# Graph attention's addend rows through DRAM instead of through TensorE, and layer norms whose squares are summed on ScalarE

## The chip, the cores and the metric

The kernel runs on one core of one Trainium2 chip. The metric is the device time of one execution in microseconds (us), as the median over several executions. No execution quoted here is over 1.5% above the fastest of its kernel, so none counts as slow. Every run was made beside runs of the kernel before on the same chip. A ratio is the mean time of one kernel's fast runs over the mean of the other's of the same rounds, so it is not quite the ratio of the medians that are quoted beside it.

## The reference

64 graphs of 256 nodes with 256 features pass through two layers; all matrices are float32. Cut to what matters here:

```python
# layer 0: two graph attentions, then a feed-forward
Wh = h @ W
e  = leaky_relu(Wh @ a[:F] + (Wh @ a[F:]).T, 0.2)      # one addend per row, one per column
att = softmax(where(adj > 0, e, -9e15), axis=1)
h = att @ Wh                                           # done twice, with W1 and W2
h = layernorm(x + h);  h = layernorm(h + relu(h @ w_ff1 + b1) @ w_ff2 + b2)
# layer 1: attention with relations, then a feed-forward
x = layernorm(h + attention(h) @ Wo + bo)
out = layernorm(x + gelu(x @ W1 + b1) @ W2 + b2)
```

So per graph there are two places where a vector of 256 addends has to lie along the columns, the same in all 128 partitions, and four layer norms.

## The kernel before

The kernel works on 32 pairs of graphs. Each pair's work is a Python generator, and three pairs are under way at once. A rule of turns decides, while the program is built, whose next piece of work is put into the engines' queues. Each `yield us, later, needs` says how long the piece lasts on TensorE, how long its results need before the way can go on, and which of three parts ("gat", "ff", "attention") it needs for itself.

```python
now, going = 0.0, []
while True:
    ...
    able = [g for g in going if alone.get(g[2]) in (None, g[0])]
    ready = [g for g in able if g[1] <= now] or [min(able, key=lambda g: g[1])]
    g = min(ready, key=lambda g: g[2] == "ff" or alone.get("ff") is g[0])
    ...
    us, later, needs = step
    now = max(now, g[1]) + us
    g[1:] = now + later, needs
```

The exponent of a sum is a product of exponentials, so a graph attention's weights need `exp(e1)` and `exp(0.2 e1)` as rows (`rise`) and the other addend as a scalar per partition (`ratio`). Before, the rows are made on TensorE: four transposes of a column that is repeated 128 times.

```python
def gat_weights(y, at, rise, ratio, adjT, empty, b):
    p = bank()
    for n in range(4):
        col = rise[:, n // 2, n % 2:n % 2 + 1]
        nc.tensor.transpose(p[:, n * P:(n + 1) * P], col.to_broadcast([P, P]), ident)   # L225
    up = work.tile([P, N], F32, name="up", bufs=2)
    nc.scalar.activation(up, p[:, :N], AF.Copy)
    ...                                    # VectorE: maximum of the two rows, mask, sums; ScalarE scales y
def add_rows(y, p, b):
    rows = y[:, of_graph(b), :].rearrange("p k d -> p (k d)")
    nc.vector.tensor_tensor(rows, p, rows, ALU.add)
def layernorm(r, gb, b):
    ...
    for j in range(2):
        nc.vector.bn_stats(st[:, j, :], r[:, 2 * b + j, :])
        nc.vector.bn_aggr(mv[:, j, :], st[:, j, :])
    nc.vector.tensor_scalar(rstd, mv[:, :, 1], EPS, None, ALU.add)
    nc.gpsimd.tensor_tensor(rstd, rstd, mhalf[:, :2], ALU.pow)
    ...
```

## Time and profile before

| | before |
|---|---|
| median of 3 runs | 3386.12 us (3384.53 to 3388.64) |
| profiled span | 3384.7 us |
| TensorE busy | 99% |
| VectorE, ScalarE, GpSimd busy | 55%, 40%, 6% |
| pair 1's first matmuls start at | 38.56 us |
| a pair's period in the steady state | 104.06 us |

The last two rows are read from TensorE's timeline, at the matmuls of `xT` with the weights (16 per pair). A pair's period is the distance between these matmuls of pair 3 and of pair 30, divided by 27. The lines of the page, of the waits and of the timelines that carry the argument are shown in the prediction. In all of them PE is TensorE, PEld its weight loads, DVE VectorE, ACT ScalarE, POOL GpSimd and SP SyncE; a letter q behind a name is the engine's sequencer, which hands it its instructions, and L225 is line 225 of that kernel's file. "Granted clock" is the clock that TensorE was given, as a share of full speed.

### The profile page before, as it was taken

Reading aid. Unit: us, or ns where it says so; the run is one execution under the profiler, and the core shown is the slowest. Engines: PE = TensorE matmul, PEld = TensorE weight load, DVE = VectorE, ACT = ScalarE, POOL = GpSimd, SP = SyncE. Lnnn points to the kernel's source line nnn. Section 1 sums busy time; section 2 is a strip of 40 time slices with the busy share of each in tenths; the row PEclk is TensorE's granted clock in tenths of the full one; section 3 lists DMA queues with packets and bytes.
Section 4 is the critical chain, followed back from the end, with each engine's and each line's share of the span. In section 5 each row is a group of like instructions: output and inputs, shape, how many; then the busy total and the mean of one; then the engine's idle time right before and its main releaser. Section 6 shows DMA issues by size and latency. Waiting matters only on the chain.

```text
span 3384.7 us, 46922 instructions
## 1 busy us (share of the span) xinstructions
PE 3335.3 (99%) x18782; PEld 2161.4 (64%) x18782; DVE 1863.3 (55%) x4833; ACT 1366.4 (40%) x2576; POOL 202.8 (6%) x262
## 2 busy tenths in 40 slices
PE   7999999999999999999999999999999999999998
PEld 5656755765676667557656756676576567665755
DVE  5646556556555555565466556555564565565454
ACT  3234434532353254245433542542354335425332
POOL 0000000000000000000000000000000000000000
PEclk9999999999999999999999999999999999999999
DMA  5000100100010001001000100010010001000000
GB/s 170 7 7 26 38 7 9 43 19 13 15 42 14 7 26 38 7 7 44 19 7 13 38 26 7 26 38 7 7 44 19 7 14 38 20 7 19 13 1 14
DMA packets 67296, 78.19 MB, mean 23 GB/s; under 512 B 3712, under 2 KB 58112, under 8 KB 67072
## 3 DMA queue, kind: packets, MB, share of 16 engines
q1 hardware_dynamic: 67072, 75.13, 7.2%
q8 instruction: 150, 2.46, 0.3%
q14 instruction: 74, 0.61, 0.1%
HBM read 58.34 MB, written 16.78 MB: 22 GB/s over the span
## 4 chain that ended last, share of the span: by engine, by line
PE 95%; ACT 4%; DMA 1%; SPq 0%; issue 0%; DVE 0%; POOL 0%; POOLq 0%; DVEq 0%
PE ps L341 26%; PE ps L330 25%; PE ps L364 7%; PE ps L410 7%; PE ps L357 6%; PE ps L382 4%; PE ps L403 4%; PE ps L253 3%; PE ps L427 3%; PE ps L279 3%; PE ps L317 3%; PE ps L267 2%; ACT L215 2%; PE ps L225 1%; ACT L333 1%; ACT xw L269 1%
## 5 line engine op out<-in xcount | busy, mean ns | idle before, releaser
L319 ACT ACTIVATE yT<-ps 128x512 f32<-128x512 f32 x192 | 113.0, 589 | 1069.7 <-PE ps L317 1069.6
L330 PE MATMUL ps<-yT,w_L_gnn_w_ff 128*128 128x512 f32 x1024 | 480.0, 601 | 0.7 <-ACT yT L319 0.7
L330 PE MATMUL ps<-yT,w_L_gnn_W 128*128 128x512 f32 x1024 | 472.4, 596 | 1.4 <-ACT yT L319 1.4
L341 PE MATMUL ps<-w_L_gnn_w_ff,ff 128*128 128x256 f32 x2048 | 458.2, 381 | 0.0
L341 PE MATMUL ps<-w_L_gnn_W,ff 128*128 128x256 f32 x2048 | 456.8, 380 | 0.0
L341 PEld LDWEIGHTS ps<-w_L_gnn_W,ff 128*128 128x128 f32 x2048 | 388.2, 190 | 65.8 <-issue 14.6
L341 PEld LDWEIGHTS ps<-w_L_gnn_w_ff,ff 128*128 128x128 f32 x2048 | 388.1, 190 | 65.8 <-issue 14.3
L396 DVE TENSOR_TENSOR m<-a,adjT 128x512 f32<-128x512 f32 x512 | 327.2, 687 | 175.4 <-ACT a L387 130.3
L302 POOL TENSOR_TENSOR rstd<-rstd,mhalf 128x2 f32<-128x2 f32 x256 | 202.1, 789 | 3175.3 <-DVE rstd L301 3161.6
L387 ACT ACTIVATE a<-ps 128x512 f32<-128x512 f32 x512 | 264.3, 603 | 232.9 <-PE ps L382 232.8
L359 DVE TENSOR_TENSOR v<-ps,b_L_gnn_bv 128x512 f32<-128x512 f32 x128 | 88.1, 689 | 464.4 <-PE ps L357 464.4
L292 DVE TENSOR_TENSOR x<-ps,x 128x512 f32<-128x512 f32 x256 | 175.8, 687 | 265.2 <-PE ps L341 142.1
L333 ACT ACTIVATE ff<-ps,c_L_gnn_b_ff 128x512 f32<-128x512 f32 x256 | 175.9, 687 | 346.0 <-PE ps L330 346.0
L330 PEld LDWEIGHTS ps<-yT,w_L_gnn_W 128*128 128x128 f32 x1024 | 185.3, 190 | 179.0 <-issue 173.7
L330 PEld LDWEIGHTS ps<-yT,w_L_gnn_w_ff 128*128 128x128 f32 x1024 | 182.1, 190 | 178.9 <-issue 175.9
L333 ACT ACTIVATE ff<-ps,c_L_gnn_b 128x512 f32<-128x512 f32 x256 | 175.7, 686 | 148.3 <-PE ps L330 146.7
L357 PE MATMUL ps<-wv,yT 128*128 128x512 f32 x512 | 235.4, 592 | 0.0
L416 DVE RECIPROCAL s<-ps 128x256 f32<-128x256 f32 x128 | 224.0, 1750 | 0.0
L232 DVE SCALAR_TENSOR_TENSOR e<-ps,ratio,up 128x256 f32<-128x256 f32 x256 | 115.8, 475 | 174.0 <-ACT up L227 174.0
L299 DVE BATCH_NORM_STATS2 st<-x 128x6 f32<-128x256 f32 x512 | 192.7, 418 | 8.7
L357 PEld LDWEIGHTS ps<-wv,yT 128*128 128x128 f32 x512 | 97.3, 190 | 122.4 <-issue 122.4
L211 DVE TENSOR_REDUCE steep<-xw 128x1 f32<-128x4 f32 x128 | 19.7, 155 | 256.8 <-ACT xw L269 211.0
(96 smaller groups left out, 4027.6 us busy)
## 6 DMA issues: line engine op xcount, KB each, us to landing
xT<-in_xT SPq DMA_DIRECT2D x32, 512.0 KB, 4.6
adjT<-in_adjT SPq DMA_DIRECT2D x32, 512.0 KB, 3.8
x<-in_x SPq DMA_DIRECT2D x32, 512.0 KB, 4.2
out<-x SPq DMA_DIRECT2D x32, 512.0 KB, 3.2
w_L_gnn_w_ff<-in_L_gnn_w_ff SPq DMA_DIRECT2D x2, 1024.0 KB, 9.4
w_L_gnn_W<-in_L_gnn_W SPq DMA_DIRECT2D x2, 1024.0 KB, 10.3
wv<-in_L_gnn_Wv SPq DMA_DIRECT2D x2, 256.0 KB, 5.0
w_L_gnn_W1T<-in_L_gnn_W1T SPq DMA_DIRECT2D x1, 256.0 KB, 2.8
```

The source lines that it names most:

```text
L292: nc.vector.tensor_tensor(rows, p, rows, ALU.add)
L299: nc.vector.bn_stats(st[:, j, :], r[:, 2 * b + j, :])
L302: nc.gpsimd.tensor_tensor(rstd, rstd, mhalf[:, :2], ALU.pow)
L330: nc.tensor.matmul(p1, lhsT=w1[:, c, m * P:(m + 1) * P], rhs=yT[:, c, :], start=c == 0, stop=c == KC - 1)
L333: nc.scalar.activation(h, p1, func, bias=b1[:, m:m + 1])
L341: nc.tensor.matmul(p2[:, j * D:(j + 1) * D], lhsT=f[m][:, k * P:(k + 1) * P], rhs=w2[:, m, :], start=m == 0, stop=m == NF - 1)
L357: nc.tensor.matmul(ps, lhsT=yT[:, c, at:at + P], rhs=wv[:, c].rearrange("p r m -> p (r m)"), start=c == 0, stop=c == KC - 1)
L364: nc.tensor.matmul(ps, lhsT=w[:, d, c * P:(c + 1) * P], rhs=yT[:, d, :], start=d == 0, stop=d == KC - 1)
L387: nc.scalar.activation(a, ps[o], AF.Exp)
L396: nc.vector.tensor_tensor(m, a, adj, ALU.mult)
L410: nc.tensor.matmul(po[o * DH:(o + 1) * DH, :N], lhsT=v[:, jc, at:at + DH], rhs=ms[o][:, jc * N:(jc + 1) * N], start=r == 0 and jc == 0, st ...
L416: nc.vector.reciprocal(s, po[:, N:])
```

## The change

The intent is to take 512 transposes and their wait off TensorE. The four exponentials of a pair are laid into 32-column blocks, VectorE transposes the blocks, a DMA of 4 KB writes them to DRAM as one row, and a second DMA of 512 KB reads that row back into all partitions. Both are issued by GpSimd. The layer norms change too: the row additions give the sums for the means, and ScalarE sums the squares. The pauses in the rule of turns are fitted to the new chain, the next pair's loads are put into the queue in layer 2 instead of layer 1, a pause precedes the last store of each pair, and `x` gets a fifth buffer.

```diff
-        nc.tensor.transpose(p[:, n * P:(n + 1) * P], col.to_broadcast([P, P]), ident)   (and the copy to up)
+        blocks = small.tile([P, 2, 32], F32, name="blocks")
+        nc.vector.transpose(blocks..., rise...)
+        row = scratch.tile([2, 16, 32], F32, name="row")                                  # in DRAM
+        nc.gpsimd.dma_start(row.rearrange("j q c -> q j c"), blocks[0:P:8])
+        rows = work.tile([P, 8, 4, 32], F32, name="rows")
+        nc.gpsimd.dma_start(rows..., row....partition_broadcast(P))
...
-            a.append(addends(y, D + 2, 0, pair, b))
-            yield 1.75, b * 1.6, None
...
-            e.append(gat_weights(y, D + 2, *a.pop(0), adjT, empty, b))
-            yield 0.5, b * 4.4, None
+            if b == 0:
+                yield 1.75, 0.0, None
+        rows, ratio = addends(y, D + 2, 0, pair)
+        yield 1.75, 8.6, None
+        e = [gat_weights(y, D + 2, rows, ratio, adjT, empty, b) for b in range(2)]
+        yield 0.0, 4.6, None
...                                                        (layer 2 likewise)
-        nc.vector.tensor_tensor(rows, p, rows, ALU.add)
+            nc.vector.scalar_tensor_tensor(row, p[...], 1.0, row, op0=ALU.mult, op1=ALU.add, accum_out=sums[:, j:j + 1])
+        nc.vector.tensor_scalar(nm, sums, -1.0 / D, None, ALU.mult)
...
-            nc.vector.bn_stats(...); nc.vector.bn_aggr(...)
+            nc.scalar.activation(aside, r[:, 2 * b + j, :], AF.Square, bias=nm[:, j:j + 1], accum_out=square[:, j:j + 1])
```

More of the change, by code (lines that the diff above doesn't have):

```diff
@@ L61, in load @@
         nc.sync.dma_start(adjT, t["adjT"][rows].rearrange("b (c p) n -> p (b c) n", p=P))
-        x = io.tile([P, 4, D], F32, name="x", bufs=4)
+        x = io.tile([P, 4, D], F32, name="x", bufs=5)
         nc.sync.dma_start(x, t["x"][rows].rearrange("b (c p) d -> p (b c) d", p=P))
@@ L76, in two_layers @@
     most = const.tile([P, NPAIR, 4], F32, name="most")
-    steep = const.tile([P, NPAIR, 4], F32, name="steep")
+    steep = const.tile([P, NPAIR, 2], F32, name="steep")
+    rises = [const.tile([P, 2, 32], F32, name=f"rise{n}") for n in range(2)]
+    for rise in rises:
+        nc.vector.memset(rise, 0.0)
     def weights(name, pool=const):
@@ L145, in two_layers @@
     small = ctx.enter_context(tc.tile_pool(name="small", bufs=6))
+    scratch = ctx.enter_context(tc.tile_pool(name="scratch", bufs=4, space=bass.MemoryType.DRAM))
     psum = ctx.enter_context(tc.tile_pool(name="psum", bufs=8, space=bass.MemoryType.PSUM))
@@ L204, in of_graph, with addends, gat_weights @@
         return slice(2 * b, 2 * b + 2)
-    def addends(y, at, layer, pair, b):
-        k = of_graph(b)
-        nc.vector.tensor_reduce(steep[:, pair, 2 * layer + b:2 * layer + b + 1], y[:, k, at:at + 2], axis=AX.XY,
-                                op=ALU.max, apply_absolute_value=True)
-        e1, e2 = y[:, k, at], y[:, k, at + 1]
-        rise, ratio = small.tile([P, 2, 2], F32, name="rise"), small.tile([P, 2], F32, name="ratio")
-        nc.scalar.activation(rise[:, 0], e1, AF.Exp, bias=shift[:, 0:1])
-        nc.scalar.activation(rise[:, 1], e1, AF.Exp, bias=shift[:, 0:1], scale=ALPHA)
-        nc.scalar.activation(ratio, e2, AF.Exp, scale=ALPHA - 1.0)
-        return rise, ratio
-    def gat_weights(y, at, rise, ratio, adjT, empty, b):
-        p = bank()
-        for n in range(4):
-            col = rise[:, n // 2, n % 2:n % 2 + 1]
-            nc.tensor.transpose(p[:, n * P:(n + 1) * P], col.to_broadcast([P, P]), ident)
-        up = work.tile([P, N], F32, name="up", bufs=2)
-        nc.scalar.activation(up, p[:, :N], AF.Copy)
+    def addends(y, at, layer, pair):
+        nc.vector.tensor_reduce(steep[:, pair, layer:layer + 1], y[:, :, at:at + 2], axis=AX.XY, op=ALU.max,
+                                apply_absolute_value=True)
+        rise, ratio = rises[layer], small.tile([P, 4], F32, name="ratio")
+        of_kind = rise.rearrange("p j (n s) -> p n j s", n=4)[:, :, :, 0]
+        for b in range(2):
+            e1 = y[:, of_graph(b), at]
+            nc.scalar.activation(of_kind[:, 2 * b], e1, AF.Exp, bias=shift[:, 0:1])
+            nc.scalar.activation(of_kind[:, 2 * b + 1], e1, AF.Exp, bias=shift[:, 0:1], scale=ALPHA)
+        nc.scalar.activation(ratio, y[:, :, at + 1], AF.Exp, scale=ALPHA - 1.0)
+        blocks = small.tile([P, 2, 32], F32, name="blocks")
+        nc.vector.transpose(blocks.rearrange("p j c -> p (j c)"), rise.rearrange("p j c -> p (j c)"))
+        row = scratch.tile([2, 16, 32], F32, name="row")
+        nc.gpsimd.dma_start(row.rearrange("j q c -> q j c"), blocks[0:P:8])
+        rows = work.tile([P, 8, 4, 32], F32, name="rows")
+        nc.gpsimd.dma_start(rows.rearrange("p q n c -> p (q n c)"), row.rearrange("j q c -> (j q c)").partition_broadcast(P))
+        return rows, ratio
+    def gat_weights(y, at, rows, ratio, adjT, empty, b):
         e = work.tile([P, 2, N], F32, name="e", bufs=4)
@@ L231, in gat_weights @@
             k = 2 * b + j
-            nc.vector.scalar_tensor_tensor(e[:, j], p[:, N:], ratio[:, j:j + 1], up, op0=ALU.mult, op1=ALU.max)
+            nc.vector.scalar_tensor_tensor(e[:, j].rearrange("p (q c) -> p q c", q=8), rows[:, :, 2 * b + 1],
+                                           ratio[:, k:k + 1], rows[:, :, 2 * b], op0=ALU.mult, op1=ALU.max)
             nc.vector.scalar_tensor_tensor(e[:, j], adjT[:, k], empty[:, k:k + 1], e[:, j],
@@ L246, in gat_layers @@
         z = work.tile([P, 4, D + 4], F32, name="xw", bufs=2)
-        a, e = [], []
         for b in range(2):
@@ L255, in gat_layers @@
                 nc.scalar.activation(y[:, k], ps[:, :D + 4], AF.Copy)
-            a.append(addends(y, D + 2, 0, pair, b))
-            yield 1.75, b * 1.6, None
-        if pair + 1 < NPAIR:
-            loaded[pair + 1] = load(pair + 1)
-        for b in range(2):
-            e.append(gat_weights(y, D + 2, *a.pop(0), adjT, empty, b))
-            yield 0.5, b * 4.4, None
+            if b == 0:
[4 more added lines that the diff above has]
+        yield 0.0, 4.6, None
         for b in range(2):
@@ L269, in gat_layers @@
                 nc.scalar.activation(z[:, 2 * b + i, :D + 2], ps[:, :D + 2], AF.Copy)
-            a.append(addends(z, D, 1, pair, b))
-            yield 1.75, 0.4 + b * 0.6, None
-        for b in range(2):
-            e.append(gat_weights(z, D, *a.pop(0), adjT, empty, b))
-            yield 0.5, b * 4.4, None
+            if b == 0:
+                yield 1.75, 0.4, None
+        rows, ratio = addends(z, D, 1, pair)
+        if pair + 1 < NPAIR:
+            loaded[pair + 1] = load(pair + 1)
+        yield 1.75, 8.6, None
+        e += [gat_weights(z, D, rows, ratio, adjT, empty, b) for b in range(2)]
+        yield 0.0, 4.6, None
         for b in range(2):
@@ L280, in gat_layers @@
                                      rhs=z[:, 2 * b + j, :D], start=j == 0, stop=j == 1)
-            add_rows(x, ps, b)
-            layernorm(x, ln[0], b)
+            layernorm(x, add_rows(x, ps, b), ln[0], b)
             if b == 0:
@@ L289, in add_rows, with layernorm @@
     def add_rows(y, p, b):
-        rows = y[:, of_graph(b), :].rearrange("p k d -> p (k d)")
-        nc.vector.tensor_tensor(rows, p, rows, ALU.add)
-    def layernorm(r, gb, b):
+        sums, nm = small.tile([P, 2], F32, name="rowsum"), small.tile([P, 2], F32, name="nm")
+        for j in range(2):
+            row = y[:, 2 * b + j, :]
+            nc.vector.scalar_tensor_tensor(row, p[:, j * D:(j + 1) * D], 1.0, row, op0=ALU.mult, op1=ALU.add,
+                                           accum_out=sums[:, j:j + 1])
+        nc.vector.tensor_scalar(nm, sums, -1.0 / D, None, ALU.mult)
+        return nm
+    def layernorm(r, nm, gb, b):
         g, beta, _ = gb
-        st, mv = small.tile([P, 2, 6], F32, name="st"), small.tile([P, 2, 2], F32, name="mv")
-        rstd = small.tile([P, 2], F32, name="rstd")
+        square, rstd = small.tile([P, 2], F32, name="square"), small.tile([P, 2], F32, name="rstd")
         for j in range(2):
-            nc.vector.bn_stats(st[:, j, :], r[:, 2 * b + j, :])
-            nc.vector.bn_aggr(mv[:, j, :], st[:, j, :])
-        nc.vector.tensor_scalar(rstd, mv[:, :, 1], EPS, None, ALU.add)
+            aside = work.tile([P, D], F32, name="aside", bufs=2)
+            nc.scalar.activation(aside, r[:, 2 * b + j, :], AF.Square, bias=nm[:, j:j + 1],
+                                 accum_out=square[:, j:j + 1])
+        nc.vector.tensor_scalar(rstd, square, 1.0 / D, EPS, ALU.mult, ALU.add)
         nc.gpsimd.tensor_tensor(rstd, rstd, mhalf[:, :2], ALU.pow)
@@ L304, in layernorm @@
             row = r[:, 2 * b + j, :]
-            nc.vector.scalar_tensor_tensor(row, row, mv[:, j, 0:1], g, op0=ALU.subtract, op1=ALU.mult)
+            nc.vector.scalar_tensor_tensor(row, row, nm[:, j:j + 1], g, op0=ALU.add, op1=ALU.mult)
         for j in range(2):
@@ L344, in feed_forward @@
                     if j == 1:
-                        add_rows(y, p2, b)
-                        layernorm(y, gb, b)
+                        layernorm(y, add_rows(y, p2, b), gb, b)
                     yield 3.44, 0.0, None
-        add_rows(y, p2, 1)
-        layernorm(y, gb, 1)
+        layernorm(y, add_rows(y, p2, 1), gb, 1)
         done_with("ff")
@@ L428, in into_rows @@
                                      start=c == 0, stop=c == KC - 1)
-            add_rows(y, ps, b)
-            layernorm(y, ln[2], b)
+            means.append(add_rows(y, ps, b))
+        means = []
         groups = [(b, c) for b in range(2) for c in range(KC)]
@@ L456, in attention @@
             divided(b, c, po)
+            if last:
+                layernorm(y, means[0], ln[2], 0)
             yield 3.1 if last else 4.1, 4.8 if last else 0.8, None
@@ L468, in attention @@
         into_rows(1)
+        layernorm(y, means[1], ln[2], 1)
         done_with("attention")
@@ L485, in whole_way @@
         yield from feed_forward(x, ff1, AF.Gelu, ln[3])
+        yield 3.44, 5.0, None
         nc.sync.dma_start(out[2 * pair:2 * pair + 2].rearrange("b (c p) d -> p (b c) d", p=P), x)
-        yield 3.44, 0.0, None
     in_turn((whole_way(pair) for pair in range(NPAIR)), 3)
-    ranges = ((reach, NPAIR * 4, N * SAFE), (most, NPAIR * 4, 1.0), (steep, NPAIR * 4, STEEP))
+    ranges = ((reach, NPAIR * 4, N * SAFE), (most, NPAIR * 4, 1.0), (steep, NPAIR * 2, STEEP))
     count = const.tile([P, len(ranges)], F32, name="count")
```

## The prediction

> **What bounds the kernel now.** I read the busy line of the page first, then the chain that ended last, then TensorE's waits, then the start and the end in the timeline.
>
> ```profile
> PE 3335.3 (99%) x18782; PEld 2161.4 (64%) x18782; DVE 1863.3 (55%) x4833; ACT 1366.4 (40%) x2576; POOL 202.8 (6%) x262
> ...
> PE 95%; ACT 4%; DMA 1%; SPq 0%; issue 0%; DVE 0%; POOL 0%; POOLq 0%; DVEq 0%
> ```
>
> TensorE is busy in all but 49.4 of 3384.7 us and carries 95% of the chain; no other engine is above 55%. A matmul's record overlaps the next one's, so busy alone does not prove a bound; the waits do:
>
> ```profile
> PE ps L225 <- ACT rise L215: 19.4, 23, 0.9
> PE pw L117 <- DVE junk L111: 7.3, 1, 7.3
> PE ps L253 <- DMA xT<-in_xT: 5.1, 1, 5.1
> PE ps L279 <- ACT xw L238: 3.3, 1, 3.3
> PE ps L267 <- ACT xw L238: 2.6, 1, 2.6
> ```
>
> Columns: total us, times, longest. All but the first line happen once, in the first 40 us; one more, 2.1 us at the first feed-forward, is left out here. So in the steady state the only thing TensorE ever waits for is the exponentials ahead of the four transposes that make the addend rows (L225). The kernel is bound by TensorE's amount of work; everything else hides behind it. So of this change only three things count: TensorE work taken away, the wait taken away, and any new wait.
>
> ```profile
> L292 DVE TENSOR_TENSOR x<-ps,x 128x512 f32<-128x512 f32 x256 | 175.8, 687 | 265.2 <-PE ps L341 142.1 <-PE ps L279 112.5 <-PE ps L427 10.1
> ...
> L299 DVE BATCH_NORM_STATS2 st<-x 128x6 f32<-128x256 f32 x512 | 192.7, 418 | 8.7
> ...
> L238 ACT ACTIVATE xw<-xw,rs 128x258 f32<-128x258 f32 (+1 forms) x256 | 115.8, 500 | 20.8 <-DVE rs L235 18.9
> ...
> L300 DVE BATCH_NORM_AGGREGATE mv<-st 128x2 f32<-128x6 f32 x512 | 77.6, 173 | 0.0
> ...
> L225 PE MATMUL ps<-ident,rise 128*128 128x128 f32 x512 | 71.3, 275 | 19.4 <-ACT rise L215 19.4
> ...
> L418 DVE SCALAR_TENSOR_TENSOR junk<-ps,s 128x256 f32<-128x256 f32 x128 | 54.3, 424 | 3.8
> ...
> L227 ACT ACTIVATE up<-ps 128x256 f32<-128x256 f32 x128 | 42.3, 379 | 3.5 <-PE ps L225 3.5
> ```
>
> ```profile
> x<-in_x SPq DMA_DIRECT2D x32, 512.0 KB, 4.2
> ```
>
> These rows (busy us, mean ns, idle before; below them a DMA's row, KB and us to landing) are the prices used below. For the start, the first pair has nothing to hide behind, and the timeline of TensorE shows it bare:
>
> ```profile
> 28.05 5.41 PE L279 MATMUL ps<-xw,e 128*128 128x256 f32 x16 [3.29 <-ACT xw L238]
> 38.56 5.38 PE L253 MATMUL ps<-w,xT 128*128 128x260 f32 x16 [5.10 <-DMA xT<-in_xT]
> ...
> 44.76 0.65 PE L225 MATMUL ps<-ident,rise 128*128 128x128 f32 x4 [0.37 <-ACT rise L215]
> 45.25 3.68 PE L157 MATMUL ps<-c_L_gnn_b_ff2c,w_L_gnn_w_ff 128*128 128x1 f32 x32
> ...
> 62.17 1.04 PE L225 MATMUL ps<-ident,rise 128*128 128x128 f32 x8
> 63.05 5.32 PE L330 MATMUL ps<-yT,w_L_gnn_w_ff 128*128 128x512 f32 x12
> ```
>
> ```profile
> 12.00:24.00 12.00, 8.81 (x44) 6.88 (x42) 4.91 (x20) 8.19 (x26) 0.00 (x0) 1.00 1.03 327
> 24.00:40.00 16.00, 7.49 (x23) 5.73 (x24) 11.63 (x38) 2.80 (x9) 1.73 (x2) 0.84 1.01 285
> 40.00:60.00 20.00, 18.94 (x84) 14.12 (x83) 8.02 (x24) 8.85 (x26) 0.00 (x0) 0.78 0.41 128
> ```
>
> The last three columns of the windows are granted clock, DMA share and GB/s: until 40 us the weights fill the DMA engines, and after idle stretches the clock falls below 1.
>
> **What the Trainium skill says.** "DMA: Bandwidth & Descriptors", section "Anatomy of one DMA — SWDGE (gpsimd) path", puts a DMA from GpSimd at about 2.0 us + bytes/436 GB/s. This kernel has none of that kind; its 512 KB loads from SyncE land in 3.8 to 4.6 us, against 3.2 us by that line, so I add one microsecond to it. The same page, "Two DMAs through the same engine are not ordered", says that a DMA reading what another wrote has to wait for the other's semaphore: the two new ones come one after the other. "ScalarE: Activation LUTs", "What ACT_TABLE_LOAD costs", gives 280 + 0.833 N ns for an ACTIVATE with a per-partition operand, 493 ns for N = 256; L238 agrees with 500 ns, and the trace's table loads agree with its 1283 ns. "TensorE: Matmul & The Clock Gate", "Part 1: The HAM clock gate", says that idle windows of about 3.4 us halve the clock; the 0.84 and 0.78 above agree.
>
> **The change part by part.**
>
> *Addend rows.* The 512 transposes and their weight loads go. The 71.3 us of the row overlap with neighbours, so I count from start to start: eight take 63.05 - 62.17 = 0.88 us, four alone 45.25 - 44.76 = 0.49 us. Summed over the whole timeline, up to the next other matmul and without waits, it is 61.2 us (between 64 x 0.88 = 56 and 128 x 0.49 = 63). With the 19.4 us of wait, 80.6 us of TensorE's time. Pair 0 lies in the start, which I count apart: 61.2 x 31/32 = 59.3, and 19.4 less its 0.31 + 0.37 = 18.7, together 78.0 us for pairs 1 to 31.
>
> In their place, once per layer and pair: five small exponentials, a block transpose on VectorE, a 4 KB DMA to DRAM, and a 512 KB broadcast back. Length of that chain after the last xw matmul, by the rows before: ACT copy 0.4, perhaps 0.3 behind other work, perhaps a table load 1.28, four exponentials at 0.2 apart 0.9, transpose about 0.3 (an estimate: 64 columns beside the 0.16 us of the smallest VectorE operations), DMA 2.0 to 2.5, broadcast 3.2 + 1 to 5: landing at 9 to 11 us. Then 2.7 us (VectorE's first row at 16.81 to TensorE at 19.55 us in the first pair) until TensorE can go on: 12 to 14 us.
>
> What lies beside it? I followed the kernel's rule of turns, old and new, only for the order of issue. In layer 1, between the new addends and the matmuls that need them stand five feed-forward blocks of four matmuls (4 x 0.433 = 1.73 us each) and two of sixteen (16 x 0.216 = 3.45): 8.7 us up to the VectorE part and 15.6 us in all. In layer 2 it is over 30 us. So the 12 to 14 us fit, with 1.6 us to spare at worst. VectorE is reached at 8.7 us and may stand in its queue until the rows land, 1 to 2 us; but there only the feed-forward runs, whose TensorE work needs no VectorE. Slip in the steady state: 2 us in all as my estimate, for 31 pairs mostly none.
>
> *Start.* Pair 0 has no cover. Before, the last xw matmul ended at 15.5 and the next matmuls began at 19.56. Now: rise 16.8, transposed 17.1, row written about 19.8, broadcast back about 25 (DMA engines full in this stretch, so 5 us), TensorE at 27.8. Second layer: matmuls until 32.5 at a lowered clock, +1.5 to rise, +0.3, DMA 2.5, broadcast 4, +2.7: 43.5 instead of 28.05. These end near 48.5, and pair 1's matmuls follow at once, for its xT, landed at 38.5, is there; before they began at 38.56. Start: +10 us, of which the lowered clock is 2.
>
> *Layer norm.* VectorE loses 192.7 + 77.6 + 175.8 us and gains 512 additions with a sum at 424 + 81 ns (the price of L418 and its accumulator read; some overlap, 0.47 apart, 241 us) and 256 small ones at 0.16 (41 us): about 160 less, to 1700. ScalarE gains 512 squares at 0.493 us, 252 us, loses 42 of `up` and some exponentials: near 1560 us, 46%, if the square needs no table of its own. None of that is on TensorE's path. The chain of one norm: before 4.0 us; now 0.94 + 0.2 + 1.1 + 0.2 + 0.8 + 0.9 = 4.2 and a hop more between engines, perhaps 4.6. The kernel leaves 6 us after each norm, so only the last ones show: +0.4 in the tail and +0.6 where the last pair has no cover.
>
> Sum: 3386.1 - 78.0 + 10 + 1 + 2 = 3321. The rounder picture, all gains and a start of only +8 with no slip, gives 3317. I put 3320.
>
> **Rivals.** (1) *A new wait in the place of the old one*: the rows land after 13 us in each pair's layer 1. Each microsecond of it costs 31 us in all; 1 us makes 3350, 2.5 us eats the gain. For it: two dependent transfers and a queue on GpSimd that also carries the norms' powers. Against: 15.6 us of cover and the diff's own pauses of 8.6 and 4.6, which look fitted. I give 15% to more than 0.5 us per pair. (2) *ScalarE becomes the brake*: squares queue ahead of evictions that TensorE needs, or the square forces table loads (512 x 1.28 us would be 657 us more). Against: 40% busy now, and TensorE never waits for ScalarE's evictions today beyond 2.1 us at L330 in the start. A few us at most; 3% for the table case, which would end near or above the old time. (3) *The norms on GpSimd wait behind the DMAs*: POOL's queue stands about 2 us between the DMAs; by the order of issue a norm follows closely only after layer 2's addends, with 4 us to the use after its own 4. Costs nothing, I think.
>
> **Range and chances.** The gain is bounded at 3386.1 - 80.6 = 3305.5. Below 3307 is hardly reachable; upward a slip of 0.6 us per pair gives 3340. So 3307 to 3340 for 8 in 10. The 2% line is near 3319, almost on my figure: faster 0.45, same 0.52, slower 0.03.
>
> **What would show it.** L225 gone, and with it the first line of the waits; PE busy near 3335 - 61 = 3274; no repeated TensorE wait on ACT xw for rows; TensorE's first pair stretched to about 48 us before pair 1; two GpSimd DMAs, 64 each, the broadcast landing in 4 to 5 us; VectorE waiting for rows 1 to 2 us per layer; squares near 0.5 us; no more table loads than 208. I am wrong if matmuls of L267's kind wait in most pairs, if pair 1 starts later than 52 us, or if ACT stands before the feed-forward's second half.

## The result, and the profile after

The kernel after takes **3364.82 us** (median of 6 runs, 3363.33 to 3366.6) beside 3386.24 us of the kernel before: ratio 0.9937, 95% interval 0.9924 to 0.995. It is faster, but by 21 us (less than 1%) in place of 66, and the time is far outside the range of 3307 to 3340.

The page of the kernel after, its busy line and its chain that ended last:

```profile
PE 3288.1 (98%) x18270; PEld 2105.2 (63%) x18270; DVE 1699.7 (51%) x4835; ACT 1524.4 (45%) x3350; POOL 275.5 (8%) x390
...
PE 78%; DVE 10%; DMA 6%; ACT 3%; issue 2%; POOL 1%; DVEq 0%; POOLq 0%; ACTq 0%
```

TensorE lost 47.2 us of busy time, and the 512 transposes are gone. But the chain now runs through VectorE, the DMAs and ScalarE for a fifth of its length; before, 95% of it was TensorE. TensorE's waits in the kernel after (total us, times, longest) say where:

```profile
PE ps L274 <- ACT xw L247: 18.5, 1, 18.5
PE ps L289 <- ACT xw L247: 14.2, 1, 14.2
...
PE ps L394 <- ACT kT L377: 6.4, 10, 2.4
PE ps L355 <- ACT ff L347: 3.7, 9, 0.7
```

The first two happen once each, in the first pair. The other two are of a kind that the kernel before did not have outside its start: TensorE waits for results of ScalarE, 19 times in all. The waits at L225, the largest of the kernel before, are gone.

The trace splits into three stretches. The predicted figures are the prediction's own: a start of 48.5, then 3336.9 us as before less 78.0, plus 2 of slip and 0.6 for the last pair, then 9.2 us as before plus 0.4.

| us | before | predicted | after | after less predicted |
|---|---|---|---|---|
| up to pair 1's first matmuls | 38.6 | 48.5 | 59.7 | +11.2 |
| from there to the start of TensorE's last matmul | 3336.9 | 3261.5 | 3287.0 | +25.5 |
| from there to the end | 9.2 | 9.6 | 14.9 | +5.3 |
| profiled span | 3384.7 | 3319.6 | 3361.6 | +42.0 |

Some 2 us more lie between the profiled run, which was the fastest of its kernel, and the median. Each of the three rows has another cause.

**The start.** TensorE's timeline in the kernel after, to be held against that of before in the prediction (start, length, line, and in brackets the idle time ahead):

```profile
34.15 5.60 PE L274 MATMUL ps<-xw,e 128*128 128x258 f32 x16 [18.52 <-ACT xw L247]
53.99 5.89 PE L289 MATMUL ps<-xw,e 128*128 128x256 f32 x16 [14.24 <-ACT xw L247]
59.72 3.67 PE L261 MATMUL ps<-w,xT 128*128 128x260 f32 x16
```

And GpSimd's timeline in the same stretch:

```profile
17.16 0.67 POOL L229 DMA_DIRECT2D row<-blocks  x1 [15.83 <-DVE blocks L227]
22.90 0.59 POOL L231 DMA_DIRECT2D rows<-row  x1 [5.07 <-DMA row<-blocks]
41.26 0.52 POOL L229 DMA_DIRECT2D row<-blocks  x1 [17.77 <-DVE blocks L227]
47.06 0.56 POOL L231 DMA_DIRECT2D rows<-row  x1 [5.28 <-DMA row<-blocks]
```

GpSimd waited 5.07 and 5.28 us for a row of 4 KB. The broadcast of layer 1, issued at 22.90, came to VectorE's first use at 31.39 us, 8.5 us later; that of layer 2, issued at 47.06, at 51.23 us. Over the whole run the page has medians of 1.9 and 3.9 us for the same two DMAs. In this stretch the DMA engines are full (a share of 1.09 from 41 to 47 us too), and TensorE's clock falls (window of the kernel after from 24 to 40 us; the last three columns are granted clock, DMA share and GB/s):

```profile
24.00:40.00 16.00, 5.60 (x16) 4.27 (x16) 4.85 (x18) 3.56 (x10) 0.00 (x0) 0.56 1.03 302
```

**The middle.** The periods of the pairs are not all alike. From pair 3 to pair 18 they are about 102.0 us, 2.0 less than before, close to the 2.5 that the prediction took (78.0 / 31). From pair 21 to pair 29 they are about 103.3, with one of 107.7. The order of TensorE's work shows why. Pair 10 first, then pair 25, both in the kernel after (L261 opens a pair, L344 and L355 are the two halves of a feed-forward of another pair, L274 is the first layer's attention):

```profile
971.43 3.67 PE L261 MATMUL ps<-w,xT 128*128 128x260 f32 x16
974.94 8.75 PE L344 MATMUL ps<-yT,w_L_gnn_w_ff 128*128 128x512 f32 x20
983.52 7.07 PE L355 MATMUL ps<-w_L_gnn_w_ff,ff 128*128 128x256 f32 x32
990.43 1.90 PE L274 MATMUL ps<-xw,e 128*128 128x258 f32 x8
```

```profile
2513.28 3.67 PE L261 MATMUL ps<-w,xT 128*128 128x260 f32 x16
2516.79 8.75 PE L344 MATMUL ps<-yT,w_L_gnn_w_ff 128*128 128x512 f32 x20
2525.37 10.52 PE L355 MATMUL ps<-w_L_gnn_w_ff,ff 128*128 128x256 f32 x48
2535.73 1.90 PE L274 MATMUL ps<-xw,e 128*128 128x258 f32 x8
```

The same five blocks of four, but then 48 matmuls in place of 32 before the attention may go on. The diff has the reason in it: the new pause is 8.6 us, and a block counts 1.72 us in the rule of turns. Five blocks are exactly 8.6. So "the pause is over" and "now" are one moment, and `g[1] <= now` is decided by the rounding of two long sums. Up to pair 20 it came out true; past a nominal time of about 2048 us, where the spacing of the numbers doubles, it came out false, and the pair goes on one block later. Running the rule alone on a computer, with the pauses of this kernel, gives the same: at pair 20 (nominal 1982 us) the pause ends 2e-13 us before "now", at pair 21 (2085 us) 9e-13 us after it. I call the two orders the first and the second.

What the second order costs is seen on ScalarE. The same place in pairs 10 and 25: the attention's rows have just been transposed, and the feed-forward's last activation (L347) is due.

```profile
1051.63 0.51 ACT L313 ACTIVATE aside<-x,nm 128x256 f32<-128x256 f32 x1 [5.90 <-DVE nm L305]
...
1053.11 0.67 ACT L347 ACTIVATE ff<-ps,c_L_gnn_b 128x512 f32<-128x512 f32 x1
```

```profile
2589.80 0.51 ACT L313 ACTIVATE aside<-x,nm 128x256 f32<-128x256 f32 x1 [6.15 <-DVE nm L305]
...
2593.55 0.51 ACT L313 ACTIVATE aside<-x,nm 128x256 f32<-128x256 f32 x1 [2.64 <-DVE nm L305]
...
2594.65 1.28 ACT L347 ACT_TABLE_LOAD   x1
2595.95 0.69 ACT L347 ACTIVATE ff<-ps,c_L_gnn_b 128x512 f32<-128x512 f32 x1
```

In the first order one norm's squares stand ahead of the activation, in the second the squares of two norms. ScalarE takes its work in order. So the activation waits until the second pair of squares has had its means from VectorE (2.64 us), and behind them for a load of its table (ACT_TABLE_LOAD, 1.28 us) which the first order does not need here: the kernel after has 150 table loads, experiment 1 with the first order throughout has 128. TensorE shows the cost. Its 16 matmuls at this place (L355, from 2593.81 us) take 4.48 us up to the next ones, against 3.45 in pair 10, with a wait of 0.36 us at 2597.75 inside, and the transposes ahead of them (L331) 0.25 us more: 1.28 us in all, nearly all of the 1.3 to 1.4 that a period of the second order is longer. In the single period of 107.7 us TensorE also waits 2.41 us for `kT` from ScalarE; after that wait the granted clock is 0.5 for 3.4 us, and four matmuls take 3.68 us in place of 1.98.

**The end.** The last output is issued at 3351.04 us, and the program ends 10.5 us later; before, from 3379.63 us, it took 5.1. The trace has the reason among the records that are not counted as busy: GpSimd's closing DRAIN, which starts once its work is done.

```
GpSimd's closing DRAIN, start us and ns:   before 3379.0   45      after 3350.22   10522
```

### The profile page after: what moved, and what is told of

Same layout as the page of the kernel before. It is cut to its first block, busy times and chain, and to the rows that moved or that the text cites.

```text
span 3361.6 us, 46862 instructions
## 1 busy us (share of the span) xinstructions
PE 3288.1 (98%) x18270; PEld 2105.2 (63%) x18270; DVE 1699.7 (51%) x4835; ACT 1524.4 (45%) x3350; POOL 275.5 (8%) x390
## 4 chain that ended last, share of the span: by engine, by line
PE 78%; DVE 10%; DMA 6%; ACT 3%; issue 2%; POOL 1%; DVEq 0%; POOLq 0%; ACTq 0%
PE ps L355 24%; PE ps L344 21%; PE ps L369 6%; PE ps L376 5%; PE ps L422 4%; PE ps L394 3%; PE ps L261 3%; PE ps L274 3%; DMA adjT<-in_adjT 3%; DVE m L408 2%; PE ps L415 2%; PE ps L439 2%; DVE s L428 2%; PE ps L289 2%; DMA rows<-row 2%
## 5 line engine op out<-in xcount | busy, mean ns | idle before, releaser
L313 ACT ACTIVATE aside<-x,nm 128x256 f32<-128x256 f32 x512 | 255.4, 500 | 695.3 <-DVE nm L305 578.2
L344 PE MATMUL ps<-yT,w_L_gnn_W 128*128 128x512 f32 x1024 | 471.6, 597 | 0.7 <-ACT yT L333 0.7
L355 PE MATMUL ps<-w_L_gnn_W,ff 128*128 128x256 f32 x2048 | 462.5, 380 | 4.6 <-ACT ff L347 3.7
L355 PE MATMUL ps<-w_L_gnn_w_ff,ff 128*128 128x256 f32 x2048 | 455.2, 379 | 0.0
L344 PE MATMUL ps<-yT,w_L_gnn_w_ff 128*128 128x512 f32 x1024 | 452.2, 594 | 0.7 <-ACT yT L333 0.7
L355 PEld LDWEIGHTS ps<-w_L_gnn_w_ff,ff 128*128 128x128 f32 x2048 | 389.0, 190 | 66.6 <-issue 15.1
L355 PEld LDWEIGHTS ps<-w_L_gnn_W,ff 128*128 128x128 f32 x2048 | 382.8, 190 | 62.4 <-ACT ff L347 11.5
L303 DVE SCALAR_TENSOR_TENSOR x<-ps,x 128x256 f32<-128x256 f32 x512 | 196.7, 413 | 338.9 <-PE ps L355 290.2
L344 PEld LDWEIGHTS ps<-yT,w_L_gnn_w_ff 128*128 128x128 f32 x1024 | 192.6, 191 | 217.7 <-issue 207.9
L344 PEld LDWEIGHTS ps<-yT,w_L_gnn_W 128*128 128x128 f32 x1024 | 183.7, 190 | 185.7 <-issue 176.2
L240 DVE SCALAR_TENSOR_TENSOR e<-rows,ratio 128x256 f32<-128x256 f32 x256 | 116.4, 477 | 333.3 <-DMA rows<-row 309.9
L347 ACT ACTIVATE ff<-ps,c_L_gnn_b_ff 128x512 f32<-128x512 f32 x256 | 175.6, 687 | 206.9 <-PE ps L344 206.9
L347 ACT ACTIVATE ff<-ps,c_L_gnn_b 128x512 f32<-128x512 f32 x256 | 173.1, 684 | 83.6 <-PE ps L344 82.2
L247 ACT ACTIVATE xw<-xw,rs 128x258 f32<-128x258 f32 (+1 forms) x256 | 117.4, 502 | 160.1 <-DVE rs L244 160.1
```

Source lines behind the costliest of these rows:

```text
L303: nc.vector.scalar_tensor_tensor(row, p[:, j * D:(j + 1) * D], 1.0, row, op0=ALU.mult, op1=ALU.add, accum_out=sums[:, j:j + 1])
L313: nc.scalar.activation(aside, r[:, 2 * b + j, :], AF.Square, bias=nm[:, j:j + 1], accum_out=square[:, j:j + 1])
L344: nc.tensor.matmul(p1, lhsT=w1[:, c, m * P:(m + 1) * P], rhs=yT[:, c, :], start=c == 0, stop=c == KC - 1)
L347: nc.scalar.activation(h, p1, func, bias=b1[:, m:m + 1])
L355: nc.tensor.matmul(p2[:, j * D:(j + 1) * D], lhsT=f[m][:, k * P:(k + 1) * P], rhs=w2[:, m, :], start=m == 0, stop=m == NF - 1)
```

## The experiments

Twelve kernels ran, in four batches, each on another chip. Each gave correct results. The kernel before had medians of 3385.19 to 3385.99 us in the batches and 3386.24 beside the kernel after, so a difference between kernels of different batches is uncertain by about 1 us more than the spread of each.

**1. The order of turns kept.** The equality is decided by a margin, nothing else is changed.

```diff
-            ready = [g for g in able if g[1] <= now] or [...]
+            ready = [g for g in able if g[1] <= now + 1e-6] or [...]
```

> The changed kernel with one edit to its rule of turns: a way counts as ready at now + 1e-6 instead of now, so that two moments that are equal but for rounding stay equal and the order of issue of pairs 3 to 20 holds to the end. Theory (order): the trace of the changed kernel shows a period of 101.9 us for pairs 3 to 18, 107.7 us once at pair 22 and 103.3 us for pairs 23 to 28; with one order all through, 10 x 1.35 + 4.4 = 18 to 20 us go, 3364.8 to about 3346 us, and every period from pair 3 on is 101.8 to 102.3 us. Rival (wear of some other kind, or the DMAs): the later periods stay at 103.3 us and the time within 3 us of 3364.8.

Measured: **3347.83 us** (3346.66 to 3349.4), ratio 0.9888, that is 17.0 us less than after. Its period is 102.02 us: 102.05 up to pair 18, 101.89 from pair 21. Of TensorE's waits for ScalarE almost nothing is left:

```profile
PE ps L394 <- ACT kT L377: 0.6, 1, 0.6
...
PE ps L355 <- ACT ff L347: 0.5, 1, 0.5
```

**2. The norms alone**, in the kernel before.

> The kernel before with the new layer norms alone (sums with the additions, squares on ScalarE, the first norm of attention moved). Theory (rows and start make the loss): within 3 us of 3386, as predicted, for TensorE's work is the same and the norms hide. Rival (ScalarE is the brake): 10 to 30 us slower, with TensorE waiting for ff or yT from ScalarE in most periods.

Measured: 3387.22 us, ratio 1.0004 (0.999 to 1.0018). The new norms neither gain nor cost there: in the steady state TensorE waits for nothing there but the exponentials of the rows, so the 148 us that VectorE saves there (1863.3 to 1715.3) have no taker.

**3. The rows alone**: the kernel after with the old norms, and with the flip of the order still in it.

> The changed kernel with the old layer norms (bn_stats and bn_aggr on VectorE) in the new places; the order of issue with its flip at pair 21 stays. Theory (start, order, end): start and end cost the same; in the second order the wait of 0.36 us for ff goes, for no square stands ahead of it, so 3355 to 3365. Rival (the norms eat the gain): 3340 or less.

Measured: 3347.76 us (3344.89 to 3349.65), ratio 0.9888. I had expected 3355 to 3365 by the theory and 3340 at most by the rival, so both numbers were missed. What it says is that the second order by itself costs little: with the old norms no squares stand in ScalarE's queue, and from pair 23 to 28 the period is 102.08 us, against 101.69 with the first order (experiment 12). The table loads are 150 here too. But ScalarE runs this one long before its activation:

```profile
2571.40 1.28 ACT L342 ACT_TABLE_LOAD   x1
2580.36 0.69 ACT L342 ACTIVATE ff<-ps,c_L_gnn_b 128x512 f32<-128x512 f32 x1 [7.68 <-PE ps L339]
```

So neither the order nor its extra table loads are enough: the 16 matmuls take 3.46 us here, and only the 0.25 us at the transposes ahead of them stay. The loss of 17 us needs both, the order and the squares.

**4. A single DMA from GpSimd** in the kernel before, read by nobody.

```diff
+    nc.gpsimd.dma_start(aside.tile([P, DH], F32, name="unread"), ones)
```

> The kernel before with a single DMA from GpSimd's queue at the start that nobody waits for. Theory (end): using GpSimd's queue at all makes the end of the program longer, 10.5 us instead of 5.1 from the issue of the last output to the last instruction, so about 5 us more, 3391 us. Rival (the end is long because of how many such DMAs there were, or by chance): within 1 us of 3386.

Measured: 3386.34 us, ratio 1.0002. GpSimd's closing DRAIN takes 140 ns. So the longer end does not come from the mere use of GpSimd's queue.

**5. Pair 0 by transposes.** To experiment 1, pair 0's rows are added in the old way, by TensorE; with this code pair 1's loads go back to their old place too.

```diff
+        e = yield from (first_layers(y, z, xT, adjT, empty) if pair == 0 else rest_layers(...))
```

> The kernel of e1_ties with pair 0 alone made by transposes on TensorE as before, all other pairs by block transpose and DMAs. Theory (start): in e1_ties pair 1's first matmuls begin at 61.9 us, before the change at 38.6; with pair 0's rows made on TensorE they begin at 38.5 to 41 us, so 19 to 22 us go: about 3327 us, with the same periods of about 102.0 us. Rival (the start's waits only move work that is waited for later, such as the weights): less than 10 us, with new TensorE waits between 40 and 110 us.

Measured: **3328.01 us** (3326.12 to 3328.55), ratio 0.9827. Pair 1 starts at 38.08 us, as in the kernel before and 23.9 us sooner than in experiment 1; 19.8 us of that show in the median. The closing DRAIN, with 124 DMAs in place of 128, takes 10.196 us: 0.0815 us less for each one, which makes 10.4 us for 128 of them. So the drain grows with the number of DMAs issued.

**6. A quiet start, first try.** To experiment 1: seven large weights, 4.75 MB, should be loaded only after pair 0's second layer. A memset of one column on VectorE was to hold each load back.

> The kernel of e1_ties with 4.75 MB of weights (both feed-forwards, Wq, Wk, Wo) loaded only after pair 0's layer 2 weights are made, so that pair 0's row DMAs do not share the DMA engines with them. Theory (start = two dependent DMAs beside the weight loads): the four DMAs of pair 0's rows, 5.1, about 8, 5.3 and 4 us to landing in the changed kernel, fall to about 2 and 4; pair 1's first matmuls begin at 46 to 53 us instead of 61.9; the time falls by 8 to 14 us, less what TensorE then waits for the weights of the first feed-forward (up to 5 us). Rival (the start is long because of the chain's fixed latency and the clock): the DMAs stay long and pair 1 begins at 58 us or later.

Measured: 3349.78 us, ratio 0.9894; pair 1 starts at 62.51 us. The edit did not do what it was for. A memset depends on nothing, so all seven ran at 1.1 us, and the loads went out from 21.9 us on. The run says nothing of the theory; experiment 9 mends it.

**7. The row DMAs from SyncE's queue**, on top of experiment 5.

```diff
-        nc.gpsimd.dma_start(row...)    nc.gpsimd.dma_start(rows...)
+        nc.sync.dma_start(row...)      nc.sync.dma_start(rows...)
```

> The kernel of e5_ties_start with the two row DMAs of each layer issued from SyncE's queue and not from GpSimd's. Theory (end): GpSimd's last drain lasts 10.52 us in the changed kernel, 0.14 with one GpSimd DMA and 0.05 without, about 0.08 us per DMA issued there; with none it is 0.05 us again and the program ends 5 us sooner than e5_ties_start, about 3322 us. The periods stay at about 102.0 us, unless loads and outputs hold the rows up in SyncE's queue. Rival (the drain belongs to the program, not to the number of GpSimd DMAs): the end stays at 10 us after the last output's issue.

Measured: **3324.65 us** (3322.79 to 3328.0), ratio 0.9818. GpSimd's drain is back at 45 ns, and from the last output's issue to the end it is 5.09 us in place of 10.38. So the longer end is the drain. Of that 5.3 us 3.4 show in the median, and the runs of the two experiments overlap (3322.79 to 3328.0 beside 3326.12 to 3328.55): that the whole gets faster by it is likely, not shown. The two DMAs land in 1.7 and 3.5 us, against 1.8 and 3.8.

**8. The second order throughout.** In the kernel after, the first pause is lengthened by a tenth of a microsecond, so the order of pair 25 holds from pair 3 on.

```diff
-        yield 1.75, 8.6, None
+        yield 1.75, 8.7, None
```

> The changed kernel with the pause after the addends of layer 1 at 8.7 instead of 8.6, nothing else: by the rule of turns the second order of issue then holds from pair 3 on. Theory (order): the period of 103.3 us, seen in the changed kernel for pairs 23 to 28 alone, holds from pair 3 on: 18 more periods at 1.2 to 1.4 us more, so 3382 to 3392 us, no gain over the kernel before (the 4.4 us of the change of order may go). Rival: within 4 us of 3365.

Measured: **3387.72 us**, ratio 1.0004: a nominal tenth of a microsecond, of which no engine ever hears, takes the whole gain. The period is 103.53 us. TensorE's waits for ScalarE now come in nearly every pair:

```profile
PE ps L394 <- ACT kT L377: 12.9, 24, 1.7
PE ps L355 <- ACT ff L347: 9.5, 26, 0.4
```

**9. A quiet start, second try.** As 6, but the column is copied from pair 0's second exponentials, so the loads must wait for them.

```diff
-            nc.vector.memset(tile_[:, 0, :1], 0.0)
+            nc.vector.tensor_copy(tile_[:, 0, :1], e[3][:, 0, :1])
             nc.sync.dma_start(tile_, w...)
```

> The kernel after with the order of turns kept, and with seven of the large weights (4.75 MB) issued only after pair 0's second layer has its exponentials: each weight tile's first column is first written by a copy that reads those exponentials, so the queue of SyncE really stands still until then. The earlier try at this used a memset, which depends on nothing and ran at 1.1 us. Theory: the row DMAs of pair 0 were slow (5.1, about 8, 5.3, about 4 us) because the weights and the prefetch behind them fill the DMA engines. Then layer 2's two DMAs fall to about 1.9 and 3.9 us, layer 1's to between that and what they were (pair 0's and pair 1's loads are still there), pair 1's first matmuls start at 47 to 54 us in place of 61.9, and the whole takes 3334 to 3342 us if the feed-forward's weights then come in time (a wait of some us at the first feed-forward would give part of it back). Rival: the two DMAs from GpSimd are slow in the start whatever else runs (a cold queue, say): start of pair 1 at 58 us or later and 3344 us or more.

Measured: 3348.23 us, ratio 0.989; pair 1 starts at 57.96 us. This time the weights were held until 52.67 us. GpSimd's timeline shows layer 2's row in a quiet stretch, and TensorE's wait for it:

```profile
43.18 0.52 POOL L234 DMA_DIRECT2D row<-blocks  x1 [16.20 <-DVE blocks L232]
45.35 0.56 POOL L236 DMA_DIRECT2D rows<-row  x1 [1.65 <-DMA row<-blocks]
```

```profile
PE ps L298 <- ACT xw L252: 10.3, 1, 10.3
```

The wait for layer 2's row fell from 5.04 us (experiment 1) to 1.65, and from transposed blocks to VectorE's first use it is 6.3 us in place of 9.7. The DMA engines' share is 0.01 from 43 to 46 us here, and 0.88 from 44 to 49 us in experiment 1. So in layer 2 the 4 KB row was slow because of what ran beside it; the rival, that DMAs from GpSimd are slow in the start whatever else runs, falls. The broadcast gained nothing (3.87 us to the first use, 3.86 in experiment 1). Layer 1 was not relieved: the loads of pairs 2 to 4 moved up into the gap, the row waited 6.52 us there, and TensorE 18.4 as before. My figure for the whole was missed. Of the 4 us gained at pair 1, 2 were lost again by pair 3, where the held weights came late, and the medians do not differ from experiment 1's. For layer 1 the contention stays argued, not shown.

**10. The best so far with the old norms**: experiment 7 without the squares.

> The best version so far (order of turns kept, pair 0 by transposes, row DMAs from SyncE: 3324.65 us, 0.9818) with the old layer norms (batch-norm statistics on VectorE, no squares on ScalarE). Theory: in the first order of turns the new norms neither cost nor gain, since neither VectorE nor ScalarE is waited for; so 3322 to 3328 us, a ratio within 0.0015 of 0.9818. Rival: VectorE's 160 us less work is worth something here, where the row chain ends on VectorE: then this run is slower, 3330 us or more.

Measured: **3316.38 us** (3316.04 to 3320.82), ratio 0.98 (0.9787 to 0.9813). I had expected no difference; it is 8.3 us less than experiment 7, and the two sets of runs do not overlap, though they come from two chips and experiment 7's runs spread over 5 us. This is the fastest kernel here: 69.6 us below the kernel before beside it (3385.99), 48.4 below after. So even in the first order the new norms cost something.

**11 and 12. The table filled.** Experiment 5 with the old norms, and experiment 1 with the old norms.

> The version with the order of turns kept and pair 0 by transposes (row DMAs from GpSimd's queue: 3328.01 us, 0.9827), with the old layer norms. It fills the fourth place of a table of two norms by two queues, of which three are measured: new norms with GpSimd's queue 3328.0, new norms with SyncE's 3324.65, old norms with SyncE's 3316.38. Theory: the new norms cost some 8 us of their own once the order is kept, whatever the queue, because VectorE then waits for ScalarE's squares in its own queue and reaches the next use late; so this run takes 3318 to 3322 us and its waits for oT fall from 4.4 to about 1.6 us. Rival: the norms are free, as the pair of runs without the new start said (3347.83 with new, 3347.76 with old), and the gain of the last run came from SyncE's queue and the old norms together, or from the chip it ran on: then 3325 to 3330 us.

> The kernel after with the old norms and with the order of turns kept: the same as the run of the rows alone (3347.76 us) but for the equality of two moments, and the same as the run with the order kept (3347.83 us) but for the norms. Theory that the new norms cost some 8 us once the order is kept: 3338 to 3342 us, and the run of the rows alone then paid about as much for its second order as the new norms cost. Rival, that the norms are free: 3345 to 3349 us.

Measured: 3321.73 us (3319.74 to 3323.54), ratio 0.9814, and 3344.98 us (3344.04 to 3346.59), ratio 0.9884. The first is what the theory of a cost of the norms said, and TensorE's waits for `oT` fall as it said, from 4.4 to 1.4 us. The second is not: it lies just below what the rival said. All in one table, in medians:

| order and start | rows from | new norms | old norms | difference |
|---|---|---|---|---|
| second order from pair 21, start as after | GpSimd | 3364.82 | 3347.76 | 17.1 |
| first order, start as after | GpSimd | 3347.83 | 3344.98 | 2.9 |
| first order, pair 0 by transposes | GpSimd | 3328.01 | 3321.73 | 6.3 |
| first order, pair 0 by transposes | SyncE | 3324.65 | 3316.38 | 8.3 |
| the kernel before (the same batch) | none | 3387.22 | 3385.19 | 2.0, not told from none |

In the three rows of the first order the new norms cost 3 to 8 us, each time between two chips. The second order costs 17.0 us with the new norms and 2.8 with the old. The cost of the norms in the first order belongs to the middle stretch: the period is 102.02 to 102.09 us with the new norms and 101.78 to 101.81 with the old. The likely way is a hop between engines that the new norm has inside: VectorE must wait for the squares before it may go on, in its own queue. That hop is argued, not tested by itself. Experiment 1's groups on VectorE, with the idle time ahead of them at the end of the line:

```profile
L319 DVE SCALAR_TENSOR_TENSOR x<-x,nm,b_L_gnn_g 128x256 f32<-128x256 f32 x256 | 123.1, 481 | 89.9 <-ACT aside L313 89.9
L319 DVE SCALAR_TENSOR_TENSOR x<-x,nm,b_L_gnn_g_ln 128x256 f32<-128x256 f32 x256 | 121.8, 479 | 49.0 <-ACT aside L313 49.0
```

With the old norms these waits are 0.0, and TensorE's wait for the attention's `oT`, which VectorE writes, falls from 3.4 to 0.9 us (experiments 1 and 12). That is half of the 4.8 us by which the middle stretch shortens between these two; the rest is spread over TensorE's modelled busy time, and I did not find it. Nor do I know why the same norms cost little or nothing in the kernel before, with the same waits on VectorE (91.6 and 87.9 us in experiment 2); that TensorE had the transposes and their own 20 us of wait there as slack is only my guess.

## Why the prediction was wrong

**The mechanism of the gain was right.** The transposes and their wait were all that could be gained, and they are gone. The row chain lands in time in the steady state: TensorE never waits for it after the first pair. In pair 10 the rows are at VectorE 8.7 us after the last matmul before them (9 to 11 predicted), and TensorE goes on 6.6 us later. The first order's period, 101.78 to 101.81 us with the old norms, comes close to 104.06 - 78.0 / 31 = 101.54. The prices fitted: squares at 500 ns against 493, VectorE at 1699.7 us busy against 1700, ScalarE at 1524.4 against 1560, two DMAs at 1.9 and 3.9 us against 2 to 2.5 and 4.2 to 5. Table loads fell from 208 to 150. One sign did not come as said: VectorE stands idle for the rows 6 to 9 us in layer 1 and not 1 to 2, but TensorE did not wait for it. TensorE is busy for 3288.1 us and not 3274, perhaps because busy time is a modelled overlap, which is why the prediction counted from start to start. But two of the three signs that the prediction named for being wrong came true: pair 1 starts later than 52 us, and ScalarE (ACT) stands before the feed-forward's second half. They lead to the steps that failed.

**"Start: +10 us" was mis-sized: +21.2.** The step that failed is "DMA 2.5, broadcast 4" beside "DMA engines full in this stretch, so 5 us". I saw that the DMA engines were full and added one microsecond for it. From transposed blocks to landed row it was 6.1 us in both layers, in place of 2.7 and 2.5, and from there to VectorE's first use 8.5 and 4.2, in place of 5.2 and 4: together some 10 of the 11.2 us over. Experiment 5 shows what the whole of it is worth, 19.8 us; experiment 9 shows for layer 2 that the other loads cause the row's delay. For layer 1 the cause stays open.

**"Slip in the steady state: 2 us in all" was wrong by the largest sum, 25.5 us.** The step is "I followed the kernel's rule of turns, old and new, only for the order of issue", worked out for one order only, and with it rival (2), "a few us at most". The order of issue is not the same in all periods, since a pause of 8.6 ties with five blocks of 1.72; the prediction had both side by side, the five blocks (8.7 us by its count) and the diff's pause, and took the pause as merely well fitted. And that ScalarE had room on average said nothing of who stands ahead of whom in its queue. (The table half of rival (2) was rightly held unlikely: with the order held, new and old norms both have 128 table loads.) By the middle stretch, 16.2 us are the second order together with the squares (3287.0 after, 3270.8 in experiment 1), 4.8 are the norms in the first order (3266.0 in experiment 12), and 4.5 remain that I cannot name.

**"+0.4 in the tail" left a term out: +5.3.** GpSimd's closing drain of 10.5 us for 128 DMAs was not on the list at all. Nothing in the profile of before could show it, since that kernel issues none from there.

**Rival (1)**, the rows late by some microseconds in each pair, was rightly held unlikely. **Rival (3)**, norms held up on GpSimd, did not show: VectorE waits 130 us in all for GpSimd's powers, 150 before. The mistake of the chances was to bound the gain from above with care and the loss only by a sum of small terms: the range of 3307 to 3340 had no room for three separate misses in one direction. Experiment 10's 3316.38 us shows that the gain was there to be had; it takes one comparison, an exception for pair 0, another queue, and leaving half of the change out. That it lies near the predicted 3320 is chance: it is another kernel.

## What to carry to other kernels

Follow a static schedule over its whole length, not for one period, and look for moments that are equal by construction: here 5 x 1.72 = 8.6 handed the order to rounding, and beside the new norms that was worth 17 us. When work moves to an engine with room, ask what stands behind it in that engine's queue and what it waits for itself, for an engine in order hands its wait on to everyone behind it. A chain of dependent DMAs that hides well in the steady state is bare in the first pair, and in layer 2 of it the other loads made the row slower still: keep the old way there, and measure the two halves of a change apart, since one of them may only cost.

## What the Trainium skill lacked or had wrong

- "VectorE: DVE Perf Modes", section "The DRAIN you can't avoid", says that the DRAINs of a program's preamble and postamble take a constant 12 ns or so on all five engines. Whether GpSimd's closing one is of that kind the trace does not say, and no page has its length: it took 45 ns with no DMA issued from its queue, 140 ns with one, 10,196 ns with 124 and 10,522 ns with 128, some 0.08 us for each. It made the end of the program 5.3 us longer (experiments 5 and 7).
- "DMA: Bandwidth & Descriptors", section "Anatomy of one DMA — SWDGE (gpsimd) path", gives 2.0 us + bytes / 436 GB/s. In the steady state that is right for 4 KB (1.9 us) and a little low for the broadcast of 512 KB (3.9 us against 3.2). The page says that the fixed part is smaller under a lighter HBM load, but not how long such a DMA takes beside full DMA engines: waits of 3.7 to 6.8 us for 4 KB in the starts of these kernels, against 1.65 in a quiet stretch of one.
- The same page, section "SWDGE vs HWDGE vs iDMA", says that SyncE's way is faster to set up. For the broadcast the runs agree, 3.5 us against 3.8 to 3.9; for the row of 4 KB they show no clear difference, 1.7 and 1.9 us (experiments 7 and 10) against 1.8 to 2.0.
- "ScalarE: Activation LUTs" counts the accumulator among an ACTIVATE's outputs and does not say what it costs. The trace has an ACTIVATION_READ_ACCUMULATOR of its own behind each square, 187 ns each, 95.6 us in all.
